# A four-layer graph network on one core: layer 3's edge numbers in fp32r, layer 0's split by a rounding copy, layer 1's norm on GpSimd

## The chip, the core and the metric

The kernel runs on one core of a Trainium2 chip. A core has five engines that each work through an instruction queue of their own, in order: PE (TensorE, matrix products into the accumulators, PSUM), DVE (VectorE, elementwise work and reductions), ACT (ScalarE, activations and copies), POOL (GpSimd, elementwise work in the on-chip memory SBUF) and SP (which starts transfers). They wait for each other by semaphores. The metric is the device time of one execution in microseconds; lower is better.

## The reference, cut to what matters

The input x is 32 graphs of 512 nodes with 128 features, and adj is one 512 x 512 matrix of zeros and ones. Each of four layers computes `x = x + layer(relu(layernorm(x)), adj)`, and layer 3 gives the result without the sum:

```python
# layer 3: every edge takes its weight from a list by its running number
m = adj > 0
idx = jnp.cumsum(m.reshape(-1).astype(jnp.int32)) - 1
vals = e[0][idx].reshape(adj.shape)          # e has 256 entries
A = jnp.where(m, vals, NEG)
A = jax.nn.softmax(A, axis=1)
out = (A * I) @ h0 + (A * (1 - I)) @ h1 + bias   # h0, h1: two projections
```

An edge number past the end of the list takes the last entry, so only the first 256 edges, counted row by row over the whole matrix, have an entry of their own. All of this depends on adj and e alone, so it is done once for all 32 graphs.

Layer 0 is an attention whose scores are built from pairs of nodes; for the nodes of the second half, its sum runs over a mask of zeros and ones. Layer 1 is an attention followed by a two-layer perceptron with norms. Layer 2 is a plain masked attention with an elu.

## The kernel before, in words

**Tiling.** A graph is four blocks of 128 nodes. Most tiles are 128 partitions by 4 x 128 values. A product of 128 x 128 by 128 x n in fp32 appears in the profile as two PE instructions. A product whose two operands are typed fp32r appears as one[...].

**The plan.** The function `tile_gnn_stack_kernel` does not emit instructions in the order of its text. It hands operations to `Plan.op`, each with an engine, an assumed length, the values it reads and writes, and, by the argument `port`, a note that DVE and POOL should not run marked instructions at the same time. `Plan.run` then chooses, step by step, the operation that can begin first by the assumed lengths, and fixes that order on every engine. A changed length, a changed number of buffers or a dropped operation can so move instructions anywhere. Buffers come from rooms (`by_pool`, `by_act`, `by_dve`, `scored`, `scores`, `turned`, `spare`, and the eight PSUM banks). The assumed lengths set the order only; on the chip, an engine runs its queue as its semaphores allow.

**The order of the work.** Per graph there is one chain of operations for each of the layers 0 to 3, with lags of 0, 4, 9 and 12 graphs, so that in the middle of the kernel four graphs are in work, one in each layer. Two more chains stand beside them: `prepare` (weights and masks) and `prepare_last` (layer 3's attention matrix), which fill gaps in the first rounds.

**The norm.** `preln(b, engine)` takes means and variances on DVE (L494, L496), the inverse deviation on POOL (`ve` L506, the power L508), and the normalised tile either on ACT (L528, with a shift made on DVE, L524) or on POOL (L543, with a shift made on ACT, L539). Then PE transposes it and ACT makes `hT`. Layers 0, 2 and 3 use POOL, layer 1 uses ACT.

**Layer 0's mask terms.** The values `hs2` have to be multiplied with the mask in fp32r, so they are split into a high and a low part, side by side in one tile `hl`. DVE cuts the last bits away (`cut`, L792), ACT copies the cut values to the high half (L805), POOL subtracts them from `hs2` for the low half (L806), and PE multiplies both halves at once (L828).

**Layer 3's preparation, `prepare_last`.**
- `up` is a triangle of ones; PE multiplies it with the transposed mask (L1106, bf16, 512 columns each), which counts the edges of a row up to each column. DVE copies the counts to `num` (L398) and a row's total to `row_n` (L1114).
- PE adds the totals of the rows before (L1121); DVE takes `row_lo` and `row_hi`, the first and last number of each row, and adds `row_lo` to `num` (L1134). From here `num` is the running number over the whole matrix.
- `in_row` says for each of the 256 list entries in which row it falls (L1159, L1160). PE gathers the numbers of these rows (`pg`, L1172). DVE compares (`ge`, L1176), takes the difference of neighbouring columns (L1181, L1182) and multiplies it with e (L1183). That is `e_at`, which holds each entry at its column.
- PE transposes `in_row` and spreads `e_at` to the rows (`pd`, L1194).
- DVE writes the last entry where the number is past the list (L1200), adds `pd` (L1204) and the mask (L1208) and takes the maximum (L1211). ACT takes the exponential (L1215), DVE divides (L1222) and takes the diagonal out (L1228 to L1230). PE transposes the result into `offT`, and the diagonal is spread into `adiag_rep`. Layer 3 uses both for every graph (L955, L970).

`e_at` and the transposed `in_row` have their place in `offT` until that is filled.

Of the kernel before, what the change touches and what calls it, by code (L numbers as in the profile page):

```python
# [37 lines left out]
P = 128  # L38
# [210 lines left out]
def kernel(  # L249
# [64 lines left out]
    scored = room("scored", 5, (P, C, P2))  # L314
    scores = room("scores", 8, (P, C, P))
    turned = room("turned", 4, (P, C, P))
    spare = room("spare", 9, (P, C, P))
# [195 lines left out]
    def preln(b, engine):  # L513
# [6 lines left out]
        if engine is ACT:  # L520
# [13 lines left out]
            op(ACT, 1.16, norm, [shift, rstd, v_x[b]], [xn])  # L534
# [135 lines left out]
    def layer0(b):  # L670
# [109 lines left out]
        def emit_rs2():  # L780
# [10 lines left out]
        cut = value(by_dve, "cut")  # L791
        op(DVE, 0.35, lambda: nc.vector.tensor_scalar(  # L792
            cut.t.bitcast(I32), hs2.t.bitcast(I32), -4096, None, ALU.bitwise_and), [hs2], [cut], port=1)
# [9 lines left out]
        for hf in range(H):  # L803
            own = slice(hf * H, hf * H + H)
            op(ACT, 0.31, lambda hf=hf, own=own: nc.scalar.copy(hl(hf)[:, :, 0, :], cut.t[:, own, :]), [cut], [hi[hf]])  # L805
            op(POOL, 0.7, lambda hf=hf, own=own: nc.gpsimd.tensor_sub(  # L806
                hl(hf)[:, :, 1, :], hs2.t[:, own, :], cut.t[:, own, :]), [hs2, cut], [lo[hf]], port=1)
# [39 lines left out]
    def layer1(b):  # L847
        hT, _ = preln(b, ACT)
        h = project_scored(hT, w1_ext, [v_w1])
        src, v_h = Value(), Value()  # L850
# [206 lines left out]
    def prepare_last():  # L1057
# [30 lines left out]

# [4 lines left out]
        for kb in range(C):  # L1093
            dve(0.31, lambda kb=kb: nc.vector.tensor_scalar(
                maskT_t(kb), adjT[:, kb, :], 0.0, None, ALU.is_gt), v_adjT, [maskT[kb]])
        num = [value(spare, "num") for _ in range(C)]
        row_n, row_lo, row_hi, nmax3, sum3, rsum3 = (
            const(n, (P, C)) for n in ("row_n", "row_lo", "row_hi", "nmax3", "sum3", "rsum3")
        )
        v_n, v_lo = Value(), Value()  # L1100
        for ib in range(C):
            pn = value(banks, "pn")

            def emit_pn(ib=ib, pn=pn):
                for kb in range(C):
                    nc.tensor.matmul(  # L1106
                        wide(pn.t), lhsT=maskT_t(kb)[:, blk(ib)],
                        rhs=up_t()[:, N - P - kb * P : 2 * N - P - kb * P],
# [3 lines left out]
            op(PE, 0.9, emit_pn, [*maskT, up], [pn])  # L1112
            copy_op(DVE, 0.6, lambda ib=ib: wide(num[ib].t), lambda pn=pn: wide(pn.t), [pn], [num[ib]])
            dve(0.1, lambda ib=ib: nc.vector.tensor_copy(row_n[:, ib : ib + 1], wide(num[ib].t)[:, N - 1 : N]),  # L1114
                [num[ib]], [v_n])
# [10 lines left out]
        op(PE, 1.5, emit_pb, [bf, v_n], [pb])  # L1126

        def emit_lo():
            nc.vector.tensor_copy(row_lo, pb.t[:, 0, 0:C])
            nc.vector.tensor_add(row_hi, row_lo, row_n)  # L1130

        dve(0.2, emit_lo, [pb, v_n], [v_lo])
        for ib in range(C):
            dve(0.31, lambda ib=ib: nc.vector.tensor_scalar(  # L1134
                wide(num[ib].t), wide(num[ib].t), row_lo[:, ib : ib + 1], None, ALU.add), [v_lo], [num[ib]])
# [18 lines left out]
        for ib in range(C):  # L1154
            ge_lo = value(spare, "ge_lo")

            def emit_in(ib=ib, ge_lo=ge_lo):
# [3 lines left out]
                    in_row_t(ib), rank, row_hi[:, ib : ib + 1], ge, ALU.is_lt, ALU.mult  # L1161
# [4 lines left out]
        e_at = offT[:, 0:KE, :]  # L1166
        in_rowT = offT[:, KE : 2 * KE, :]
        v_e_at, v_in_rowT = [Value() for _ in range(KE)], [Value() for _ in range(KE)]
        for kb in range(KE):
            pg = value(banks, "pg")  # L1170
            for ib in range(C):
                op(PE, 0.86, lambda kb=kb, ib=ib, pg=pg: nc.tensor.matmul(  # L1172
                    wide(pg.t), lhsT=in_row_t(ib)[:, blk(kb)], rhs=wide(num[ib].t),
                    start=(ib == 0), stop=(ib == C - 1)), [in_row[ib], num[ib]], [pg])
            ge = value(spare, "ge")
            dve(0.6, lambda kb=kb, pg=pg, ge=ge: nc.vector.tensor_scalar(  # L1176
                wide(ge.t), wide(pg.t), next_k[:, kb : kb + 1], None, ALU.is_ge), [pg, v_next], [ge])

            def emit_e(kb=kb, ge=ge):
                g = wide(ge.t)  # L1180
# [114 lines left out]
```

## Time and profile before

Three runs took 1076.15, 1074.54 and 1074.25 us; the median is 1074.54.

| | us |
|---|---|
| median of the runs | 1074.54 |
| profiled execution | 1074.58 |
| its span, first to last instruction | 1072.5 |
| PE busy | 1042.8 |
| DVE busy | 891.1 |
| ACT busy | 800.1 |
| POOL busy | 740.1 |

How to read the lines. A group line names the source line, the engine, the operation, the tile it writes and the tiles it reads, the shapes and the count; then the busy time in us and the mean of one in ns; then the idle time of the engine just before these instructions, and what ended it. A chain line has a start in us, a length in us, an engine, a tile and a line: the chain follows the work that ended last back from the end, at each step to what released it. PE products are pipelined and their ends are modelled, so a PE that is busy all the time is not of necessity at its peak, and the distance between starts says more than the length of one.

### The profile page before, as it was taken

The page shows a single profiled execution, that of the slowest core. Times are in us where ns is not written, and L with a number is a line of the kernel's source. Part 1 is how long each engine was busy: PE and PEld are TensorE (multiplying, and loading weights), DVE is VectorE, ACT ScalarE, POOL GpSimd, SP SyncE. Part 2 cuts the span into 40 slices and gives each one's busy share as a digit, 9 for nine tenths or more (in the row PEclk, how much of TensorE's full clock was granted, in tenths as well). Part 3 has the DMA queues.
Part 4 walks back from the last instruction along what each step waited for, and adds up shares of the span by engine and source line. Part 5 has one row for each costly group of instructions (what it writes and reads, how often), then busy time and mean ns, then how long its engine had stood idle before and what let it go on. Part 6 is the DMA issues. An engine that isn't in the chain of part 4 may idle for free.

```text
span 1072.5 us, 24953 instructions
## 1 busy us (share of the span) xinstructions
PE 1042.8 (97%) x8333; PEld 953.6 (89%) x8333; DVE 891.1 (83%) x3772; ACT 800.1 (75%) x2068; POOL 740.1 (69%) x1040
## 2 busy tenths in 40 slices
PE   6899999999999999999999999999999999999996
PEld 5786888889899999999999999999998999999995
DVE  7999999999988888888888889888887877876562
ACT  3577779887877777887777788877777878777571
POOL 7467546778677778877777787777767766657544
PEclk8899999999999999999999999999999999999998
DMA  7300000000000000000000000000000000000000
GB/s 183 82 1 2 1 2 11 12 11 21 2 21 21 21 21 21 21 1 21 21 21 11 12 11 2 12 11 11 11 11 11 12 9 13 11 11 16 16 25 25
DMA packets 56910, 20.47 MB, mean 19 GB/s; under 512 B 21584, under 2 KB 56272, under 8 KB 56784
## 3 DMA queue, kind: packets, MB, share of 16 engines
q1 hardware_dynamic: 56784, 18.90, 7.4%
q8 instruction: 66, 1.08, 0.4%
q14 instruction: 60, 0.49, 0.2%
HBM read 10.43 MB, written 8.39 MB: 18 GB/s over the span
## 4 chain that ended last, share of the span: by engine, by line
PE 77%; DVE 14%; ACT 3%; SPq 2%; POOL 2%; DMA 2%; issue 1%; DVEq 0%; ACTq 0%; POOLq 0%
PE po L658 18%; PE pt L405 14%; PE po L970 11%; PE pg L897 8%; PE proj L578 6%; PE po L823 4%; PE prow L405 3%; PE p L564 3%; PE po L966 3%; PE px L564 3%; DVE y L605 2%; PE pz L564 2%; DVE st L494 2%; PE po L828 2%; DVE pT L647 2%; SPq L389 1%
## 5 line engine op out<-in xcount | busy, mean ns | idle before, releaser
L658 PE MATMUL po<-h,pT 128*128 128x128 f32 x2048 | 240.8, 275 | 0.3
L658 PEld LDWEIGHTS po<-h,pT 128*128 128x128 f32 x2048 | 234.4, 192 | 1.5 <-ACT pT L396 0.5
L543 POOL TENSOR_SCALAR xn<-xs,shift,rstd 128x128 f32<-128x128 f32 x384 | 179.2, 480 | 11.4 <-ACT shift L539 9.6
L638 ACT ACTIVATE y<-y,nmax 128x512 f32<-128x512 f32 x256 | 181.6, 713 | 2.6 <-DVE nmax L620 2.2
L508 POOL TENSOR_TENSOR rstd<-ve,mhalf 128x4 f32<-128x4 f32 x160 | 166.0, 1038 | 13.3
L605 DVE CUSTOM_DVE_ANT_0 y<-prow,bias 128x512 f32<-128x512 f32 x256 | 163.1, 683 | 2.2 <-PE prow L405 2.2
L970 PE MATMUL po<-h,offT 128*128 128x128 f32 x1024 | 136.0, 276 | 0.7 <-ACT h L396 0.7
L897 PE MATMUL pg<-adjTe,hg 128*128 128x512 f32 x256 | 131.2, 594 | 0.4 <-DVE ge L1176 0.4
L405 PE MATMUL pt<-ident,y 128*128 128x128 f32 x1024 | 129.2, 273 | 1.9 <-ACT y L638 1.6
L405 PEld LDWEIGHTS pt<-ident,y 128*128 128x128 f32 x1024 | 115.2, 141 | 17.7 <-ACT y L638 9.8
L970 PEld LDWEIGHTS po<-h,offT 128*128 128x128 f32 x1024 | 125.1, 193 | 1.2 <-ACT h L396 1.2
L494 DVE BATCH_NORM_STATS2 st<-xs 128x6 f32<-128x128 f32 x512 | 110.2, 276 | 5.6 <-POOL xs L948 2.8
L578 PE MATMUL proj<-w_ext,hT 128*128 128x130 f32 x768 | 103.8, 278 | 1.4 <-ACT hT L553 1.4
L578 PEld LDWEIGHTS proj<-w_ext,hT 128*128 128x128 f32 x768 | 95.5, 192 | 9.5 <-issue 4.8
L630 ACT ACTIVATE y<-y,src 128x512 f32<-128x512 f32 x128 | 85.3, 717 | 22.4 <-DVE rmax L605 18.3
L843 POOL TENSOR_TENSOR xs<-xs,rest 128x256 f32<-128x256 f32 x32 | 23.5, 736 | 113.3 <-DVE top L616 82.3
L553 ACT ACTIVATE hT<-pt 128x512 f32<-128x512 f32 x128 | 75.0, 590 | 33.3 <-PE pt L405 18.4
L396 ACT COPY h<-proj 128x260 f32<-128x260 f32 x192 | 66.1, 372 | 32.1 <-PE proj L578 30.2
L630 ACT ACTIVATE y<-y,h 128x512 f32<-128x512 f32 x128 | 82.6, 713 | 7.4 <-DVE rmax L605 7.3
L405 PE MATMUL pt<-ident,xn 128*128 128x128 f32 x512 | 79.4, 275 | 6.8 <-POOL xn L543 6.3
L647 DVE TENSOR_TENSOR pT<-pt,adjT 128x512 f32<-128x512 f32 x128 | 83.4, 677 | 1.5 <-PE pt L405 1.5
L405 PEld LDWEIGHTS pt<-ident,xn 128*128 128x128 f32 x512 | 61.5, 141 | 25.7 <-POOL xn L543 10.1
(189 smaller groups left out, 2331.5 us busy)
## 6 DMA issues: line engine op xcount, KB each, us to landing
xs<-in_x_dram SPq DMA_DIRECT2D x32, 256.0 KB, 3.9
out_dram<-yo SPq DMA_DIRECT2D x32, 256.0 KB, 2.3
u<-h SPq DMA_DIRECT2D x128, 0.5 KB, 1.8
bias<-in_adj_dram SPq DMA_DIRECT2D x4, 256.0 KB, 4.0
wts<-in_L_gnn_W_dram SPq DMA_DIRECT2D x3, 64.0 KB, 3.8
rows<-in_L_gnn_bias_dram SPq DMA_DIRECT2D x2, 64.0 KB, 3.7
wt_o<-L_gnn_others_weight_dram SPq DMA_DIRECT2D x1, 64.0 KB, 2.6
wts<-n_L_gnn_self_weight_dram SPq DMA_DIRECT2D x1, 64.0 KB, 4.1
```

Of the source, the lines that this page charges most:

```text
L405: nc.tensor.transpose(dst(k), src(k), ident)
L494: nc.vector.bn_stats(st[:, c, :], src(c))
L508: nc.gpsimd.tensor_tensor(rstd.own, ve, mhalf, ALU.pow)
L543: nc.gpsimd.tensor_scalar(xn.t[:, c, :], src[:, c, :], shift.own[:, c : c + 1], rstd.own[:, c : c + 1], ALU.add, ALU.mult,)
L578: nc.tensor.matmul(p[:, c, :], lhsT=column(hT, 2 * k + c), rhs=w_ext, start=True, stop=True)
L605: nc.vector.tensor_tensor_reduce(wide(y[ib].t), wide(prow.t), bias[:, ib, :], 1.0, LOWEST, ALU.add, ALU.max, rmax.own[:, ib : ib + 1],)
L630: nc.scalar.activation(yw, yw, AF.Prelu, alpha=0.2, bias=src()[:, ib : ib + 1])
L638: nc.scalar.activation(yw, yw, AF.Exp, bias=nmax.own[:, ib : ib + 1], accum_out=ssum[0].own[:, ib : ib + 1])
L647: op(DVE, 0.6, lambda ib=ib, pt=pt, pT=pT: nc.vector.tensor_mul(pT.t, pt.t, weights[:, :, blk(ib)]), [pt, *v_weights], [pT])
L658: nc.tensor.matmul(po[ib].t[:, ib, :], lhsT=pT.t[:, jb, :], rhs=h[0].t[:, jb, 0:P], start=(jb == 0), stop=(jb == C - 1),)
L897: nc.tensor.matmul(wide(pg.t), lhsT=hg.t[:, nb, :], rhs=adjTe[:, nb, :], start=(nb == 0), stop=(nb == C - 1))
L970: nc.tensor.matmul(po[ib].t[:, ib, :], lhsT=offT[:, jb, blk(ib)], rhs=h1.t[:, jb, :], start=False, stop=(jb == C - 1),)
```

## The change

- **Layer 3's numbers stay within their row.** `num` is no longer made a running number over the whole matrix. `row_lo` goes into the thresholds instead: a new small product `pk` brings each entry's `row_lo` to `first_k`, against which the gathered counts are compared, and `last_lo` is the row's own threshold for the last entry. Counts within a row are at most 512.
- **Single fp32r passes.** `num`, `in_row`, `e_at` and the transposed `in_row` are written as fp32r, and the gathering and spreading products run in it. So that e keeps its precision it is split in two terms, `e_hi` and `e_lo`, and the spreading product runs over both. The counting product streams only the columns that the triangle doesn't leave at zero.
- **Other engines.** ACT copies `num` out of PSUM. POOL takes the difference of neighbouring columns (into `adiag_rep`, which is free until the end) and adds the mask. Adding `pd` and taking the maximum are one DVE instruction. The softmax is built in `offT`, not in `num`, and `e_at` and the transposed `in_row` have tiles of their own in `spare`.
- **Layer 0.** The cut on DVE goes. ACT's copy to fp32r reads `hs2` itself and rounds, and POOL subtracts the rounded values.
- **Layer 1.** `preln` is called with POOL. The value `v_h` holds its tile's buffer.
- **Rooms.** `scored` has 6 buffers instead of 5, `spare` 8 instead of 9. Some assumed lengths differ.

```diff
-    scored = room("scored", 5, (P, C, P2))
+    scored = room("scored", 6, (P, C, P2))
...
-    spare = room("spare", 9, (P, C, P))
+    spare = room("spare", 8, (P, C, P))
...
-            op(ACT, 1.16, norm, [shift, rstd, v_x[b]], [xn])
+            op(ACT, 1.54, norm, [shift, rstd, v_x[b]], [xn])
...
-        cut = value(by_dve, "cut")
-        op(DVE, 0.35, lambda: nc.vector.tensor_scalar(
-            cut.t.bitcast(I32), hs2.t.bitcast(I32), -4096, None, ALU.bitwise_and), [hs2], [cut], port=1)
...
-            op(ACT, 0.31, lambda hf=hf, own=own: nc.scalar.copy(hl(hf)[:, :, 0, :], cut.t[:, own, :]), [cut], [hi[hf]])
+            op(ACT, 0.31, lambda hf=hf, own=own: nc.scalar.copy(hl(hf)[:, :, 0, :], hs2.t[:, own, :]), [hs2], [hi[hf]])
             op(POOL, 0.7, lambda hf=hf, own=own: nc.gpsimd.tensor_sub(
-                hl(hf)[:, :, 1, :], hs2.t[:, own, :], cut.t[:, own, :]), [hs2, cut], [lo[hf]], port=1)
+                hl(hf)[:, :, 1, :], hs2.t[:, own, :], hl(hf)[:, :, 0, :].bitcast(F32)), [hs2, hi[hf]], [lo[hf]], port=1)
...
     def layer1(b):
-        hT, _ = preln(b, ACT)
+        hT, _ = preln(b, POOL)
         h = project_scored(hT, w1_ext, [v_w1])
-        src, v_h = Value(), Value()
+        src, v_h = Value(), Value(h[0].slot)
...
                     nc.tensor.matmul(
-                        wide(pn.t), lhsT=maskT_t(kb)[:, blk(ib)],
-                        rhs=up_t()[:, N - P - kb * P : 2 * N - P - kb * P],
+                        wide(pn.t)[:, kb * P :], lhsT=maskT_t(kb)[:, blk(ib)],
+                        rhs=up_t()[:, N - P : 2 * N - P - kb * P],
...
-            copy_op(DVE, 0.6, lambda ib=ib: wide(num[ib].t), lambda pn=pn: wide(pn.t), [pn], [num[ib]])
+            copy_op(ACT, 0.59, lambda ib=ib: num_t(ib), lambda pn=pn: wide(pn.t), [pn], [num[ib]])
...
-        for ib in range(C):
-            dve(0.31, lambda ib=ib: nc.vector.tensor_scalar(
-                wide(num[ib].t), wide(num[ib].t), row_lo[:, ib : ib + 1], None, ALU.add), [v_lo], [num[ib]])
+            nc.vector.tensor_scalar(last_lo, row_lo, -1.0, NE + 1.0, ALU.mult, ALU.add)
...
+        def emit_terms():
+            nc.vector.tensor_copy(e_hi, e_col)
+            nc.vector.tensor_sub(e_lo, e_col, e_hi.bitcast(F32))
...
+        def emit_pk():
+            for kb in range(KE):
+                for ib in range(C):
+                    nc.tensor.matmul(
+                        pk.t[:, 0, kb : kb + 1], lhsT=in_row_t(ib)[:, blk(kb)], rhs=row_lo[:, ib : ib + 1],
+                        start=(ib == 0), stop=(ib == C - 1),
+                    )
...
+                    nc.tensor.matmul(
+                        wide(pg.t), lhsT=in_row_t(ib)[:, blk(kb)].bitcast(F32R), rhs=num_t(ib),
+                        start=(ib == 0), stop=(ib == C - 1),
+                    )
...
-                wide(ge.t), wide(pg.t), next_k[:, kb : kb + 1], None, ALU.is_ge), [pg, v_next], [ge])
-
-            def emit_e(kb=kb, ge=ge):
-                g = wide(ge.t)
-                nc.vector.tensor_copy(e_at[:, kb, 0:1], g[:, 0:1])
-                nc.vector.tensor_sub(e_at[:, kb, 1:], g[:, 1:], g[:, 0 : N - 1])
-                nc.vector.tensor_scalar(e_at[:, kb, :], e_at[:, kb, :], e_col[:, kb : kb + 1], None, ALU.mult)
+                wide(ge.t), wide(pg.t), first_k[:, kb : kb + 1], None, ALU.is_ge), [pg, v_first], [ge])
+
+            def emit_at(ge=ge):
+                nc.gpsimd.tensor_copy(adiag_rep[:, 0:1], wide(ge.t)[:, 0:1])
+                nc.gpsimd.tensor_sub(adiag_rep[:, 1:], wide(ge.t)[:, 1:], wide(ge.t)[:, 0 : N - 1])
+
+            def emit_e(kb=kb):
+                for t, e in enumerate((e_hi.bitcast(F32), e_lo)):
+                    nc.vector.tensor_scalar(e_at_t(t, kb), adiag_rep, e[:, kb : kb + 1], None, ALU.mult)
...
+                for t in range(2):
+                    for kb in range(KE):
+                        nc.tensor.matmul(
+                            wide(pd.t), lhsT=wide(in_rowT[kb].t).bitcast(F32R)[:, blk(ib)], rhs=e_at_t(t, kb),
+                            start=(t == kb == 0), stop=(t == 1 and kb == KE - 1),
+                        )
...
+            def emit_mask(ib=ib):
+                a = offT[:, ib, :]
+                nc.gpsimd.tensor_add(a, a, bias[:, ib, :])
...
+                nc.vector.tensor_tensor_reduce(a, wide(pd.t), a, 1.0, LOWEST, ALU.add, ALU.max, top)
+                nc.vector.tensor_scalar(nmax3[:, ib : ib + 1], top, -1.0, None, ALU.mult)
```

## The prediction

> **What bounds the kernel now.** I read the page first (engine totals), then the table of busy time by stretch, then the chain of work that ended last, then the groups of instructions inside the stretch that the chain points to.
>
> ```profile
> PE 1042.8 (97%) x8333; PEld 953.6 (89%) x8333; DVE 891.1 (83%) x3772; ACT 800.1 (75%) x2068; POOL 740.1 (69%) x1040
> ```
>
> PE at 97% suggests that only PE work counts. The stretches (columns: length, then busy time and instruction count of PE, PEld, DVE, ACT, POOL, the granted clock, DMA) say when that is so:
>
> ```profile
> 40.00:160.00 120.00, 115.32 (x794) 95.36 (x794) 117.49 (x505) 86.85 (x247) 68.01 (x95) 0.97 0.04 6
> 160.00:300.00 140.00, 138.47 (x1100) 125.30 (x1100) 130.62 (x579) 118.64 (x318) 103.78 (x146) 1.00 0.06 15
> 300.00:800.00 500.00, 500.00 (x4123) 466.47 (x4123) 421.18 (x1824) 397.09 (x1031) 374.15 (x514) 1.00 0.06 14
> 1000.00:1072.50 72.50, 61.97 (x512) 58.92 (x510) 33.83 (x109) 30.29 (x69) 36.24 (x54) 0.94 0.08 23
> ```
>
> From 300 to 800 us PE never pauses; 4123 instructions in 500 us are 8.25 per us. From 40 to 160 us it runs 6.6 per us, and DVE is the fuller engine: 117.5 of 120 us. That is the stretch in which layer 3's preparation runs between the first batches. The chain there, a few of its pieces in order of time:
>
> ```profile
> 126.03 0.60 DVE num L1204
> ...
> 128.51 0.60 DVE num L1208
> ...
> 133.97 0.60 DVE nmax L1211
> ...
> 138.87 0.33 DVE cut L792
> ```
>
> Adding the chain's pieces by engine in the six stretches of 20 us from 40 to 160 gives DVE 15.5, 18.3, 18.1, 13.8, 20.2 and 14.0: 99.9 of 120 us. Preparation and cuts stand in it. So the kernel has a start whose last wait is DVE's, a long middle that is PE's alone, and a tail of 72.5 us with PE 85% busy. Before 40 us the chain is DMA and SP's queue.
>
> **Part 1: layer 3's edge numbers, PE.** Rates come from the chain at 300 us:
>
> ```profile
> 300.20 0.86 PE pg L897 x2
> 301.06 0.44 PE prow L405 x4
> 301.50 0.48 PE po L828 x4
> ```
>
> A 512-column fp32 product is two instructions, 0.86 us. Four 256-column fp32r products take 0.48, so 0.12 each, 0.47 ns per column; 512 columns then cost 0.24 (estimate from that row). The gathering product (L1172): 8 x 0.86 = 6.9 becomes 8 x 0.24 = 1.9, so -5.0. The spreading product (L1194): 6.9 becomes 16 x 0.24 = 3.8, because e is split in two terms, so -3.0. The counting product (L1106) streams 1280 columns per row block in place of 2048: 16 x 192 x 0.47 ns = -1.4, at 20 to 28 us, under the DMA chain. Added: 8 one-column fp32 products (pk), 16 instructions; nearest row the one-column products at L1121, 20 in 2.3 us, so +1.8. Sum -7.6, of which -6.2 in the stretch from 40 to 160.
>
> **Part 2: the same, DVE, ACT, POOL.** The rows, taken from 20 to 160 us:
>
> ```profile
> L792 DVE TENSOR_SCALAR cut<-hs 128x512 int32<-128x512 int32 x9 | 3.7, 416 | 0.0
> L1208 DVE TENSOR_TENSOR num<-num,bias 128x512 f32<-128x512 f32 x4 | 2.7, 680 | 0.0
> L1211 DVE TENSOR_REDUCE nmax<-num 128x1 f32<-128x512 f32 x4 | 2.7, 678 | 0.0
> L1134 DVE TENSOR_SCALAR num<-num,row_lo 128x512 f32<-128x512 f32 x4 | 2.4, 613 | 0.0
> L1182 DVE TENSOR_TENSOR offT<-ge 128x511 f32<-128x511 f32 x2 | 2.4, 1182 | 0.0
> ```
>
> Off DVE go L1134 (2.4), L1182 with its first-column copy L1181 (2.4 + 0.3), L1208 (2.7) and L1211 (2.7): 10.5. On come two more products with e (0.486 each by L1183: 1.0), the add that becomes add-with-maximum (L605: 0.683 + 0.082 for its read-out, against 0.670: +0.4 over four), four negations of one column (0.154 by L1018: 0.6), and four small ones (last_lo, first_k, the two terms, about 0.16 each: 0.6): 2.6. The copies out of PSUM (L398, 4 x 0.678 = 2.7) move to ACT at 4 x 0.59, but at 30 to 35 us, where ACT was 45% busy and the chain is DMA's; I count nothing for them, and up to 2.7 if DVE's queue carries its lead past 40 us.
>
> POOL gets four mask adds (1.28 each, as L958) and two differences with their first column (1.28 + 0.3): 8.3 us. They lie on the way from ge to e_at and from num to the softmax; POOL was 57% busy there. Should that cover go, layer 3 starts late, but it is first needed at 245.7 us, by layer 3's own-term product on DVE (L955), some 80 us behind.
>
> **Part 3: the cut in layer 0.** Eight cuts lie in 40 to 160: 8 x 0.416 = -3.3 on DVE. ACT's rounding copy takes the place (0.402, as before, now from hs2), and POOL's subtraction now waits for ACT instead of DVE. Behind that POOL instruction stand, by the order, a batch's four norm pieces and hn's add; PE's mask products wait for it. Between nothing and one ACT activation (0.72) per batch; I take 0, since the copy can start 0.4 earlier than before.
>
> **Part 4: layer 1's norm.** ACT loses 4 x 0.485 per batch and gains a shift of 0.20; DVE loses its shift (6 x 0.163 = 1.0 in the stretch); POOL gains 4 x 0.48 = 1.92.
>
> ```profile
> L543 POOL TENSOR_SCALAR xn<-xs,shift,rstd 128x128 f32<-128x128 f32 x384 | 179.2, 480 | 11.4 <-ACT shift L539 9.6 <-DVE res L923 1.2
> L528 ACT ACTIVATE xn<-xs,shift,rstd 128x128 f32<-128x128 f32 x128 | 52.5, 485 | 1.4 <-PE px L564 0.8 <-DVE shift L524 0.6
> ```
>
> In the middle a round of the four layers takes 31.03 us (in the chain, a group of layer 1's third products begins at 338.95 and the next one at 369.98 us). POOL: 374.15/500 x 31.03 = 23.2, plus 1.92, is 25.1; DVE 26.1 falls to 25.6; ACT 24.6 to 22.9. Nobody reaches 31.03, so nothing is charged there. Cover gone, 1 us of late norm per round would be 1 us of PE.
>
> [...] By the rows: DVE's two-SBUF-input update L924 takes 0.695 on average, its PSUM-fed product L647 0.677; 0.02 apart, with POOL 57 to 75% busy, and the plan keeps marked instructions of the two apart. I charge 1 us of the 10.7, and keep it for the range.
>
> The room changes (scored 6, spare 8) cost nothing by themselves; the instructions of the start come in another order, and PE's last 136 products stand in the same order as before, so I let the tail keep its length.
>
> **The sum.** DVE in the stretch: -10.5 + 2.6 - 3.3 - 1.0 = -12.2, so 117.5 becomes 105.3. PE: 115.3 - 6.2 = 109.1 by busy time[...]. Two engines this full do not interleave perfectly; the stretch now lasts 2.5 over its fuller engine. DVE 105.3 + 2.5 + 1 (port) = 109; PE's own bound is about the same. 120 - 109 = 11; I take off 1 for the reordered start. The profiled execution was 1074.58 (span 1072.5 and 2.08 around it), 0.04 over the median, which changes nothing: 1074.5 - 10 = 1064.5.
>
> **Rivals.** *Both shares count in part* (15%): PE's saving alone converts, or half of DVE's, because latencies fill the holes: 3 to 6 us, about 1070. For: PE stands at 115 of 120 too. Against: the chain there is 83% DVE.
> *More* (8%): the 3.1 us taken from DVE at 20 to 40 us move the start as well, and the stretch from 160 to 300, DVE at 93%, shortens: 1058.
> *No change* (8%): [...]12.2 - 10.7 = 1.5 us left: 1073.
> *Slower* (8%): layer 1's norm becomes late in the middle. It stands in POOL's in-order queue with two other batches' norms and behind their power instructions (1.04 each); where it ends after PE reaches its transposes, PE stops in every round. 0.7 us in each of 32 rounds is 22, less the 10: 1087. It decides from 0.3 us per round. Against: from 300 to 800 PE waited for no POOL norm, though three layers take theirs from it, and POOL idles 5 us per round for layer 0's rest.
>
> **How the numbers follow.** My own case (the stretch gives 6 to 14 us: 1060.5 to 1068.5) has 61%. Faster: 61 + 15 + 8 = 84%. A measurement of this kernel tells 0.2% (2.1 us) from no change; within that 8%, slower 8%. The range runs from 1058.5, half of *more*, to 1072.5, all of *in part*, and leaves out *slower*, most of *no change* and the far end of *more*: 20%.
>
> **What would show it.** After: gathering and spreading products in single instructions of 0.24 spacing; DVE without L1134, L1208, L1211 and cuts; the stretch between the first layer-0 products and PE's saturation shorter by about 10; the same 31.03 us round in the middle, without PE waits on xn; POOL near 81% there. Wrong if PE shows idle time before layer 1's transposes, if two-input DVE rows grow beyond 0.7, or if the start is as long as now with DVE below 95%.

## The result and the profile after

The changed kernel takes 1075.51 us (median of 12 runs, 1071.82 to 1077.78); the kernel before takes 1074.29 (12 runs, 1073.12 to 1076.15). The ratio is 1.0005 with a 95% interval of 0.9992 to 1.0019: no difference that can be measured. The prediction was 1064.5, with a range of 1058.5 to 1072.5. It was wrong: the gain of 10 us didn't come. The changed kernel also spreads more than the one before: its single runs differ by 6 us.

The profiled execution of the changed kernel took 1077.78 us, with a span of 1076.0, and is the slowest of its twelve. Three lines of its page: the engine totals, the granted clock of TensorE in 40 slices, and the chain by engine.

```profile
PE 1045.5 (97%) x8341; PEld 965.0 (90%) x8341; DVE 871.7 (81%) x3702; ACT 763.4 (71%) x1976; POOL 796.4 (74%) x1176
...
PEclk8698999999999999999999999999999999999998
...
PE 85%; POOL 5%; DVE 5%; issue 2%; ACT 1%; DMA 1%; SPq 0%; POOLq 0%; DVEq 0%; ACTq 0%
```

The clock and the chain of the kernel before:

```profile
PEclk8899999999999999999999999999999999999998
...
PE 77%; DVE 14%; ACT 3%; SPq 2%; POOL 2%; DMA 2%; issue 1%; DVEq 0%; ACTq 0%; POOLq 0%
```

DVE has 19 us less to do (891.1 before) and POOL 56 us more (740.1 before). In the chain, DVE's share falls from 14% to 5%, and PE and POOL have taken its place. The second digit of the clock is new. It was 8 before and is 6 now: between 27 and 54 us the trace has TensorE at half of its clock for 20.5 us (27.0 to 40.6 and 47.5 to 54.3).

The table of busy time by stretch, as it was shown of before (length, busy time and count of PE, PEld, DVE, ACT, POOL, granted clock, DMA share, GB/s):

```profile
40.00:160.00 120.00, 111.29 (x794) 98.11 (x794) 111.15 (x505) 79.71 (x234) 88.72 (x126) 0.94 0.03 4
160.00:300.00 140.00, 139.87 (x1119) 127.33 (x1118) 129.12 (x556) 114.03 (x301) 110.61 (x160) 1.00 0.06 14
300.00:800.00 500.00, 499.98 (x4113) 466.25 (x4112) 413.28 (x1787) 375.01 (x978) 387.77 (x577) 1.00 0.06 14
1000.00:1076.00 76.00, 64.91 (x529) 61.31 (x527) 36.38 (x115) 33.23 (x75) 37.41 (x54) 0.95 0.07 22
```

From 40 to 160 us no engine is full any more: PE is at 111.3 (115.3 before) and DVE at 111.2 (117.5 before). Yet just as many PE instructions pass as before, 794. A part of what was taken off the two engines has become idle time on both. In the middle, PE is as full as before, with 4113 instructions per 500 us (4123 before).

The tail is longer. The last 502 PE instructions, in the kernel before and then in the changed one:

```profile
1001.70:1072.50 70.80, 60.27 (x502) 57.70 (x500) 33.14 (x108) 28.59 (x65) 35.52 (x54) 0.94 0.08 23
```

```profile
1003.60:1076.00 72.40, 61.31 (x502) 58.19 (x501) 34.30 (x108) 29.63 (x67) 36.68 (x54) 0.95 0.08 23
```

Both do the same products, and the changed kernel takes 1.6 us more for them.

The prices of the single instructions were right. Of the changed kernel, the groups from 20 to 160 us, and one piece of its chain:

```profile
L1249 POOL TENSOR_TENSOR offT<-offT,bias 128x512 f32<-128x512 f32 x4 | 5.1, 1271 | 0.4 <-DVE offT L1243 0.4
...
L1254 DVE CUSTOM_DVE_ANT_0 offT<-pd,offT 128x512 f32<-128x512 f32 x4 | 2.7, 684 | 0.0
...
L1212 POOL TENSOR_TENSOR adiag_rep<-ge 128x511 f32<-128x511 f32 x2 | 2.1, 1035 | 0.0
```

```profile
97.88 0.94 PE pd L1235 x4
```

Four spreading products take 0.94, so 0.235 each (0.24 foretold); POOL's mask add takes 1.271 (1.28), its difference 1.035 (1.28), and the add with maximum 0.684 (0.683).

What PE waits for in the changed kernel from 40 to 160 us, from the view of waits (line, what it waited for, us in all, times, the longest):

```profile
PE po L825 <- POOL hl L803: 1.9, 3, 1.5
PE prow L405 <- DVE ltn L737: 1.6, 1, 1.6
PE prow L405 <- DVE ls L695: 1.4, 1, 1.4
PE pt L405 <- POOL xn L543: 1.2, 3, 0.7
```

And a part of its chain, where POOL carries it:

```profile
67.41 1.40 POOL hl L803 x2
68.80 1.74 POOL xn L543 x4
70.54 1.24 POOL offT L1249
71.78 1.96 POOL xn L543 x4
73.74 0.70 POOL xs L840
...
81.22 0.70 POOL hl L803
...
81.96 1.48 PE po L825 x4
```

POOL, to which the prediction gave its new work for nothing, is busy 19.50 of the 20 us from 60 to 80. Its queue holds the norms, the new mask adds and layer 0's low halves one behind the other, and at 80.45 us PE stands still for 1.5 us until the last of these is there. That made three suspects: POOL's queue; the order, which the plan chose anew; and the clock, which the trace records as granted at half for 34.1 us before 100 us (13.7 us in the kernel before). Half clock for 20.5 us more is 10.2 us of TensorE's full speed, about the size of the gain that is missing. But this profile is of the slowest run, and its mean clock, 0.980, is the lowest of the twelve. Their average is 0.986, that of the kernel before 0.991 in its runs beside the experiments: on the average run, 0.005 of 1075 us, some 5 us of full speed.

### The profile page after: what moved, and what is told of

Its sections match the earlier page's. It is cut to its first block, busy times and chain, and to the rows that moved or that the text cites. A ratio compares the mean times of both kernels' runs of the same rounds, so it can differ in the third digit from the quotient of the medians.

```text
span 1076.0 us, 24957 instructions
## 1 busy us (share of the span) xinstructions
PE 1045.5 (97%) x8341; PEld 965.0 (90%) x8341; DVE 871.7 (81%) x3702; ACT 763.4 (71%) x1976; POOL 796.4 (74%) x1176
## 4 chain that ended last, share of the span: by engine, by line
PE 85%; POOL 5%; DVE 5%; issue 2%; ACT 1%; DMA 1%; SPq 0%; POOLq 0%; DVEq 0%; ACTq 0%
PE po L658 20%; PE pt L405 16%; PE po L967 10%; PE pg L894 9%; PE proj L578 7%; PE po L820 5%; PE prow L405 3%; PE p L564 3%; PE po L825 2%; PE px L564 2%; PE pz L564 2%; PE po L963 2%; POOL xn L543 2%; PE po L817 1%; PE po L830 1%
## 5 line engine op out<-in xcount | busy, mean ns | idle before, releaser
L543 POOL TENSOR_SCALAR xn<-xs,shift,rstd 128x128 f32<-128x128 f32 x512 | 230.9, 466 | 2.8 <-PE pt L405 1.2
L508 POOL TENSOR_TENSOR rstd<-ve,mhalf 128x4 f32<-128x4 f32 x160 | 169.7, 1061 | 13.3
L405 PE MATMUL pt<-ident,y 128*128 128x128 f32 x1024 | 133.8, 275 | 0.5 <-DVE pT L647 0.2
L578 PEld LDWEIGHTS proj<-w_ext,hT 128*128 128x128 f32 x768 | 99.4, 197 | 17.7 <-issue 9.0
L578 PE MATMUL proj<-w_ext,hT 128*128 128x130 f32 x768 | 106.1, 282 | 1.9 <-ACT hT L553 1.7
L939 POOL TENSOR_TENSOR v<-v,rows 128x512 f32<-128x512 f32 x32 | 40.8, 1274 | 71.4 <-DVE v L938 71.4
L945 POOL TENSOR_TENSOR xs<-xs,em 128x512 f32<-128x512 f32 x32 | 41.9, 1309 | 69.4 <-DVE em L944 63.3
L405 PE MATMUL pt<-ident,xn 128*128 128x128 f32 x512 | 82.2, 279 | 7.2 <-POOL xn L543 6.2
L396 ACT COPY h<-proj 128x260 f32<-128x260 f32 x192 | 65.0, 371 | 20.5 <-PE proj L578 18.1
```

The source lines that it names most:

```text
L405: nc.tensor.transpose(dst(k), src(k), ident)
L508: nc.gpsimd.tensor_tensor(rstd.own, ve, mhalf, ALU.pow)
L543: nc.gpsimd.tensor_scalar(xn.t[:, c, :], src[:, c, :], shift.own[:, c : c + 1], rstd.own[:, c : c + 1], ALU.add, ALU.mult,)
L578: nc.tensor.matmul(p[:, c, :], lhsT=column(hT, 2 * k + c), rhs=w_ext, start=True, stop=True)
```

## The experiments

Times are medians. Ratios are to the kernel before, run beside each on the same chip (1074.08 to 1074.33 us).

### Parts taken back, or made alone

Each of the first two runs is the changed kernel with one part taken back; the third takes back both, which leaves layer 3's part and the rooms; the fourth is the kernel before with the norm and the rooms only.

```diff
 # e1: layer 1's norm back on ACT
-        hT, _ = preln(b, POOL)
+        hT, _ = preln(b, ACT)
 # e2: layer 0's cut back on DVE (cut, L792; ACT and POOL take cut again)
+        op(DVE, 0.35, lambda: nc.vector.tensor_scalar(
+            cut.t.bitcast(I32), hs2.t.bitcast(I32), -4096, None, ALU.bitwise_and), [hs2], [cut], port=1)
...
 # e3: both of these edits to the changed kernel
 # e4: the kernel before, with
+    scored = room("scored", 6, (P, C, P2))
+    spare = room("spare", 8, (P, C, P))
...
+        hT, _ = preln(b, POOL)
...
+        src, v_h = Value(), Value(h[0].slot)
```

> The changed kernel with one word put back: layer 1's norm on ACT (as before), layer 3's and layer 0's parts as changed. Theory POOL: between 40 and 110 us the changed kernel's POOL is the fullest engine (19.5 of 20 us at 60 to 80), and the norm's pieces are 14 of its 30 there; without them POOL has room, the start no longer runs late, and the time falls to 1066 +- 2. Theory clock: what cost the gain is TensorE at half clock for 34 us of the first 100 us (14 us before), made by gaps that any reordered start has; then the half-clock time stays near 30 us and the time near 1074.[...]

> The changed kernel with layer 0's cut on DVE put back, the norm on POOL and layer 3's part as changed. Theory POOL: the norm stays, so no gain: 1075 to 1078 (DVE has its 0.42 per graph again, hidden). A theory that the rounding copy, and POOL's wait for ACT behind it, ate the gain: 1066.

> Layer 3's part and the rooms alone: norm on ACT and cut on DVE as before. Theory POOL: 8.3 us of new POOL work in the start (mask adds, differences) against 10.7 us of norm that are gone; DVE loses 7.9 us and PE 7.6: 1068 +- 2. Theory clock or reordering: 1072 to 1076, with over 25 us at half clock in the first 100.

> The kernel before with layer 1's norm on POOL (its tile held, scored 6 and spare 8 as in the change), nothing else changed. Theory POOL: the norm alone makes the start longer and nothing else shorter: 1077 to 1081, POOL over 85% busy at 60 to 100 us. Theory clock: 1074 unless the half-clock time in the first 100 us grows over 14 us. If moving the norm is harmless: 1074.

| | us | ratio, interval |
|---|---|---|
| norm back on ACT | 1093.76 | 1.0193 [1.0168, 1.0218] |
| cut back on DVE | 1094.14 | 1.0184 [1.0171, 1.0197] |
| layer 3's part alone | 1092.02 | 1.0164 [1.0151, 1.0177] |
| norm alone | 1078.29 | 1.0041 [1.0028, 1.0055] |

All four are slower than both kernels. The profiled execution of the last run took 3799 us, far from its other five, so only its times are read. No expectation named a number near 1092. The fourth's 1077 to 1081 came true, but by luck: the rooms alone, without the norm, take 1079.99 (below).

No part has a price of its own here: all three together cost nothing, any two or one of them up to 20 us. Putting the cut back, 0.416 us of DVE's work for each graph and 3.3 in the start, can't cost 18.6 us by the work in it; from 300 to 800 us PE waits for nothing in that run. Each version gets a new order from the plan, and the orders differ by more than the work does. Where the norm is back on ACT, a part of the loss lies in the middle: from 300 to 800 us PE is busy 497.8 and 496.5 us. With the cut back, one wait in the first 160 us is longer than the whole edit there. The view of waits of that run:

```profile
PE pk L1189 <- DVE in_row L1163: 4.8, 1, 4.8
```

The plan has put the new small product `pk` (L1186 in the changed kernel) so early on PE's queue that everything behind it stands for 4.8 us.

### The order alone

The kernel before with nothing but the new rooms: every instruction is the same, only their order differs.

```diff
-    scored = room("scored", 5, (P, C, P2))
+    scored = room("scored", 6, (P, C, P2))
...
-    spare = room("spare", 9, (P, C, P))
+    spare = room("spare", 8, (P, C, P))
...
-        src, v_h = Value(), Value()
+        src, v_h = Value(), Value(h[0].slot)
```

> The kernel before with only the buffer counts of the change (scored 6, spare 8, layer 1's tile held by the added value): no instruction added or removed, only the plan's order differs. Theory order (the plan's order alone moves the time by more than the work that the change takes away): more than 4 us off 1074. If order is harmless: 1074 +- 1.

It took 1079.99 us, ratio 1.0049 [1.0036, 1.0061]: 5.7 us for the order alone. Its stretch from 40 to 160 us, and its largest wait there:

```profile
40.00:160.00 120.00, 109.42 (x753) 89.50 (x752) 117.12 (x495) 81.92 (x236) 70.24 (x95) 0.99 0.03 4
```

```profile
PE po L823 <- DVE hs L788: 5.6, 3, 3.0
```

DVE is as full as in the kernel before (117.1 against 117.5), but 753 PE instructions pass in place of 794. The same view of the kernel before has this wait at 2.2 us:

```profile
PE po L823 <- DVE hs L788: 2.2, 2, 1.3
```

DVE's busy time is the same in both; what differs is the order of its queue, and with it how long PE waits for `hs`. The clock isn't the cause: before 100 us this run has 10.2 us at half clock, the kernel before 13.7. So a full DVE doesn't say how long the stretch is.

### The work alone

The other way round: the order of the kernel before, kept on every engine, with the work left out that the change removes. DVE's adds of `row_lo` and of the mask, the maximum (one column each in their place), the differences and layer 0's cuts are gone, and three of four gathering and one of two spreading products. The output is then not the reference's.

```diff
-                wide(num[ib].t), wide(num[ib].t), row_lo[:, ib : ib + 1], None, ALU.add), [v_lo], [num[ib]])
+                wide(num[ib].t)[:, 0:1], wide(num[ib].t)[:, 0:1], row_lo[:, ib : ib + 1], None, ALU.add), [v_lo], [num[ib]])
...
-                op(PE, 0.86, lambda kb=kb, ib=ib, pg=pg: nc.tensor.matmul(
+                op(PE, 0.86, lambda kb=kb, ib=ib, pg=pg: ib == 0 and nc.tensor.matmul(
...
```

> The order of the kernel before, instruction for instruction on every engine, with the work that my sum takes away left out. On DVE the running-number add, the mask add and the maximum run over one column, the column difference and layer 0's cut are left out: about 12 us less in 40 to 160 us. On PE 10 of the 16 gathering and spreading products are left out, 8.6 us. The output is not the reference's. Theory sum (the accounting is right and the new order is what failed): 1064 +- 3. Theory that the start is bound by latencies and not by DVE's and PE's amounts of work: above 1070.

It took 1070.85, ratio 0.9966 [0.9954, 0.9979]. By the prediction's own sum this kernel should have won 10 to 12 us; it won 3.5. Its stretch from 40 to 160 us:

```profile
40.00:160.00 120.00, 110.15 (x785) 94.26 (x784) 111.70 (x508) 88.86 (x251) 67.10 (x98) 0.96 0.04 6
```

The clock there is nearly that of the kernel before (0.97), and neither engine is full. Nothing was added to POOL or ACT here and nothing was moved, so most of the missing gain isn't the price of what the change adds.

### The clock

The changed kernel, its order kept, with filler products (128 x 128, values never read) ahead of its three pauses of 1.4 to 1.5 us: before `pc_w` at 25.3, before graph 4's `prow` at 47.3, and before graph 4's mask products at 80.5 us. The first of them, from the view of waits of the changed kernel (the other two are shown above):

```profile
PE pc_w L416 <- issue: 1.5, 1, 1.5
```

```diff
+    def fill(own, n=5):
+        for _ in range(n):
+            nc.tensor.matmul(own, lhsT=ident, rhs=ident, start=True, stop=True)
...
+            if b == 4:
+                fill(prow.t[:, 0, :])
```

> The changed kernel in its own order, with five filler products (0.22 us each) put on PE ahead of each of three waits in the start: before the score-weight product at 25 us, before layer 0's row transposes of graph 4 at 47 us and before its mask products at 80 us; their results are overwritten. Theory clock (pauses of 1.4 us at these places drop TensorE to half clock for 6.8 us each): half-clock time in the first 100 us falls from 34 to below 20 us and the time by 4 to 8, to 1068 to 1071. Theory POOL: 3.3 us more PE work or nothing, 1075 to 1078.

It took 1070.40 (1070.01 to 1071.12), ratio 0.9960 [0.9948, 0.9973]: 5.1 us less than the changed kernel, though PE does 3.3 us more. It is the fastest version here that leaves no work out, ahead of both kernels. The half clock before 100 us is 6.8 us in its profile, 34.1 in that of the changed kernel. The stretches of the changed kernel, and then of this one:

```profile
20.00:40.00 20.00, 18.20 (x102) 17.13 (x101) 15.80 (x90) 9.19 (x27) 15.24 (x30) 0.67 0.62 150
40.00:60.00 20.00, 17.46 (x120) 16.24 (x119) 17.17 (x89) 11.04 (x41) 10.69 (x17) 0.81 0.05 2
60.00:80.00 20.00, 18.79 (x147) 16.97 (x146) 20.00 (x99) 12.39 (x38) 19.50 (x29) 1.00 0.08 15
80.00:100.00 20.00, 17.93 (x114) 15.84 (x114) 16.74 (x72) 12.77 (x37) 17.78 (x28) 0.83 0.01 1
```

```profile
20.00:40.00 20.00, 19.23 (x150) 17.91 (x147) 18.24 (x108) 11.07 (x34) 18.39 (x34) 0.91 0.69 151
40.00:60.00 20.00, 17.33 (x133) 15.29 (x133) 19.69 (x104) 12.96 (x50) 14.51 (x22) 1.00 0.05 2
...
80.00:100.00 20.00, 18.67 (x124) 15.23 (x125) 19.84 (x89) 12.82 (x34) 19.33 (x31) 1.00 0.02 2
```

PE looks busy in both, 18.2 and 19.2 of 20 us from 20 to 40; but at a clock of 0.67 the first gets through 102 instructions and the second through 150, ten of them the five fills. Busy time at half clock is little more than half work: the 16 products `proj` from 28.74 us take 3.67 us in the changed kernel, at half clock, and 2.03 from 29.38 us in the kernel before, at full clock.

How much of the 5.1 us is the clock's can be read from the runs as well. Within the twelve runs of the changed kernel the time falls by 5.35 us for each 0.01 of mean clock (1077.78 at 0.980, 1071.82 at 0.990; correlation -0.73). Their mean is 0.986, that of the five runs with fills 0.9934, so 0.0074 more, which by this slope is 4.0 us. That is a correlation and an estimate, but it needs no other version.

The control is the kernel before with 18 fillers at three of its own pauses:

```diff
+                if ib == 0 and b in (1, 3,):
+                    fill(own)
...
+            if first_fill:
+                fill(pt.t[:, 0, :], 8)
```

> The kernel before, with every engine's order kept, and 18 filler products of 128 x 128 (about 4 us of PE, values never read) ahead of three of its pauses: the first transposes of layer 0 (2.54 us at 12.0) and the second and fourth graph's products with hs (1.29 us at 44.2, 0.91 at 62.1). Theory 'the half clock that the changed kernel's early pauses draw is what the change lost': the kernel before has 13.7 us at half clock in its start, of which the fills can take at most 6.8 us of capacity; I expect 1071 to 1073, and never as much as the 5.1 us that the fills brought in the changed kernel. Rival 'fills make any order of this kernel about 4 us faster': 1070, the same as the changed kernel with its fills, and then the change itself is worth nothing even at a full clock.

1073.89 (13 runs), ratio 0.9996 [0.9987, 1.0004]: nothing that can be measured. Neither number that the expectation gave was right. So fills don't make any order 4 or 5 us faster. But the control moves the clock only a little. The mean clock of its runs is 0.9926, that of the kernel before beside them 0.9904: 0.0022 more, where the fills of the changed kernel brought 0.0074. Its profiled execution, with 3.4 us at half clock in the start in place of 13.7, is one of its fast ones: 1072.47, 2.1 us less than the profiled one of the kernel before. So it isn't shown that the clock is worth nothing in the kernel before; that kernel has less of it to win back.

### POOL

The changed kernel in its order, with POOL relieved of some 15 us in the start: the first six norms of layer 1 computed by ACT at the same place of the plan, and the mask adds on one column. The values are then not the reference's.

```diff
-        hT, _ = preln(b, POOL)
+        hT, _ = preln(b, POOL, b < 6)
...
-                nc.gpsimd.tensor_add(a, a, bias[:, ib, :])
+                nc.gpsimd.tensor_add(a[:, N - 1 :], a[:, N - 1 :], bias[:, ib, N - 1 :])
```

> The changed kernel in its own order, with POOL's new work in the start taken off its queue: the norm pieces of layer 1's first six graphs are issued to ACT at the same place (with a shift that is not scaled, so their values are not the reference's), and the mask adds run over one column. POOL loses 15 us in the first 200. Theory POOL (POOL at 19.5 of 20 us holds the start): 1066 to 1070. Theory clock: what the pauses do, so near 1075 if the pauses at 25, 47 and 80 us stay.

1074.65 (13 runs), ratio 1.0000 [0.9991, 1.0009]. POOL falls from 19.50 to 12.69 of 20 us between 60 and 80, and the time stays. POOL carried the chain there, but it isn't what the gain was lost to: the half clock from 27 to 41 us, which comes before it, stands in this run as in the changed kernel (a mean clock of 0.67 from 20 to 40 us in both). The one from 81.6 us is gone (1.00 from 80 to 100 us, against 0.83). What POOL's work would cost at a full clock was not run.

### Which engine's saving counts

The order of the kernel before, 31 filler products at five pauses, and the work left out on both engines, on DVE alone, and on PE alone (the outputs are then not the reference's, as in the run with the work left out).

```diff
+                if ib == 0 and b in (1, 3, 5,):
+                    fill(own)
...
+                if b == 0 and nb == 0:
+                    fill(pg.t[:, 0, :], 8)
...
```

> The kernel before in its own order with the work of the change left out (as in the run of that name: about 12 us of DVE's work and 8.6 us of PE's; the output is then not the reference's), and 31 filler products (about 7 us of PE) ahead of its pauses at 12.2, 42.8, 59.4, 83.7 and 100.5 us. It took 1070.85 without the fills. Theory 'the work taken out turned into waits between engines, and those waits have no clock to win back': 1069 to 1071. Rival 'the sum was right and the half clock ate it': 17 us at half clock are 8.5 us of capacity, so 1063 to 1066.

> The kernel before in its own order, with the 31 filler products at five pauses and only DVE's work left out (about 12 us, layer 3's adds, differences and maximum and layer 0's cuts; the output is then not the reference's). With DVE's and PE's work out and the same fills it took 1068.75, 5.3 below the kernel before. The prediction's rule (the stretch lasts 2.5 us over its fuller engine, and DVE is the fuller one): with PE's products back PE's busy time is the bound, and about 4 us are won, 1070. 'DVE's saving alone carries it': 1069, the same as with both. 'PE's saving alone carries it': 1073 to 1074, the same as the fills alone.

> The same order and fills, with only PE's products left out (three of four gathering and one of two spreading products, 10 of 512 columns, about 8.6 us of PE; the output is then not the reference's), and all of DVE's work in place. The prediction's rule (DVE was the fuller engine) gives nothing over the fills alone: 1073.9. 'PE's saving carries it': 1069. If each of the two alone brings 2 to 3 us, the stretch is bound by chains in which both engines take turns, and neither engine's total tells its length.

| left out, with fills | us | ratio, interval | less than the fills alone |
|---|---|---|---|
| nothing (the 18 fills of the control) | 1073.89 | 0.9996 [0.9987, 1.0004] | |
| 8.6 us of PE | 1072.81 | 0.9989 [0.9981, 0.9997] | 1.1 |
| 12 us of DVE | 1070.85 | 0.9965 [0.9953, 0.9977] | 3.0 |
| both | 1068.75 | 0.9950 [0.9936, 0.9964] | 5.1 |

The stretch from 40 to 160 us of the run with DVE's work out, then of the one with both out:

```profile
40.00:160.00 120.00, 119.12 (x861) 101.34 (x860) 112.61 (x515) 89.46 (x253) 68.73 (x101) 0.99 0.04 6
```

```profile
40.00:160.00 120.00, 114.88 (x852) 99.17 (x851) 114.50 (x516) 91.83 (x259) 69.83 (x103) 0.99 0.04 6
```

The first row has 18 fills and the others 31, since the control was not run with 31. Neither saving counts in full. DVE's alone gives 3.0 us, a quarter. PE's alone, 1.1, isn't clear of the noise, as its interval overlaps that of the fills alone; with DVE's work already out, PE's products bring another 2.1 (1070.85 to 1068.75). With DVE's work alone out PE is busy 119.1 of 120 us, some 5 us of it with fills, so the fills may hide a part of what DVE's saving is worth. The two single runs lie near what the expectations worked out from the prediction's rule (1070 and 1073.9) and don't refute it; the run with both out and no fills does. With both out and fills, 1068.75 is just below the 1069 to 1071 of the first theory and far from its rival's 1063 to 1066.

With both out and fills, the clock is at 0.99 and both engines stand at 114 to 115 of 120 us, so neither is full. What is left are short waits in many places. The largest of PE and of DVE there:

```profile
PE prow L405 <- ACT h L396: 1.2, 2, 0.7
```

```profile
DVE hn L897 <- POOL rstd L890: 1.9, 3, 1.2
```

### What holds the clock down

In the kernel before, TensorE's clock falls to half at 43.26 us and is back at 50.09. PE had not paused since 38.26 us. Its instructions ahead of the fall, from the view of them in order of time:

```profile
38.75 0.60 PE L405 MATMUL prow<-ident,ls 128*128 128x128 f32 x4
39.19 2.29 PE L1121 MATMUL pb<-row_n,bf 128*128 128x1 f32 x20
41.34 1.14 PE L578 MATMUL proj<-w_ext,hT 128*128 128x130 f32 x8
42.31 1.47 PE L405 MATMUL pt<-ident,xn 128*128 128x128 f32 x4
```

The 20 products `pb` (L1121 before, L1123 after) are one column wide. In the changed kernel they lie at 32.2 to 36.5 us, within the 13.7 us at half clock. That they bring the clock down like a pause was a guess. Two more runs of the changed kernel in its order test it: with eight fills between these products only, and with the fills at the three pauses as well.

```diff
             for ib in range(C):
+                fill(pb.t[:, 1, :], 2)
                 for kb in range(ib + 1):
```

> The changed kernel, every engine's order kept, with 8 filler products of 128 x 128 (about 1.8 us of PE at full clock, values never read) between the 20 one-column products pb at 32 to 36 us, and none at the pauses. Theory 'one-column products count as idle for the clock': the half clock that the pause at 25.3 us starts at 27.0 ends at 33.8 in place of 40.6 (6.8 us in place of 13.7), and the time falls by 0 to 2 us below the changed kernel's, to 1073.5 to 1075.5. Rival 'only the pauses count': the 13.7 us stay, and the time rises by up to 1.8 us.

> The changed kernel with fills at its three pauses, as in the earlier run (1070.40), and between the 20 one-column products as well. Theory 'one-column products count as idle for the clock': the 3.4 us at half clock that followed those products at 33.2 us in the earlier run are gone, only the first one near 16 us stays; the time is 1069 to 1071, since the fills cost 1.8 us of PE and give back 1.7. Rival 'only the pauses count': the half clock at 33 us stays, as nothing paused before it, and the time is 1071 to 1072.

With fills in `pb` alone, half clock takes 3.4 us of the stretch from 27 to 41 us in place of 13.6 (clock 0.76 and 1.00 of 7 us each, against 0.50 and 0.53). The table of busy time of the changed kernel, then of that run:

```profile
27.00:34.00 7.00, 7.00 (x35) 7.00 (x35) 5.82 (x32) 4.33 (x11) 4.01 (x7) 0.50 0.73 189
34.00:41.00 7.00, 7.00 (x35) 7.00 (x36) 3.29 (x14) 0.20 (x1) 5.57 (x11) 0.53 0.43 94
```

```profile
27.00:34.00 7.00, 6.78 (x47) 6.81 (x47) 5.94 (x37) 4.80 (x14) 5.59 (x11) 0.76 0.76 179
34.00:41.00 7.00, 6.94 (x61) 6.75 (x61) 5.00 (x21) 1.18 (x3) 5.51 (x10) 1.00 0.41 90
```

The expectation was 6.8 us, so a part of the fall is more than its theory gives; these are single profiles. The runs agree: the mean clock of the 14 with fills in `pb` is 0.9908, that of the changed kernel's 0.986. With the fills at the pauses alone, the clock is 0.94 from 27 to 34 us and 0.81 from 34 to 41; with all fills it is 1.00 in both, but 0.94 from 40 to 60 and 0.97 from 60 to 80 us, where it was 1.00. So fills between these products took half clock away there in both runs. Why they do was not shown.

For the time it is worth little. With fills in `pb` alone it is 1074.03, ratio 0.9998 [0.9988, 1.0008], not to be told from the changed kernel: the eight fills are about 1.8 us of PE, and take up most of what the clock gives back. With all fills it is 1071.64, ratio 0.9980 [0.9971, 0.9989], 1.2 us more than with the fills at the pauses alone. Its mean clock, 0.9928, is no higher than the 0.9934 there, so these fills cost their time and give nothing back.

## Why the prediction was wrong, point by point

- **The prices of the instructions: right.** Single passes at 0.235, the rows gone from DVE, POOL's new pieces at or below their price.
- **"The stretch now lasts 2.5 over its fuller engine": this step failed.** It took a nearly full DVE for a bound that moves as DVE's work shrinks. In the old order, at nearly the old clock, 12 us of DVE and 8.6 us of PE gave 3.5 us, not 11; with the fills in both, 5.1. The chain, 83% DVE, named the engine that is late most often, but a queue in a fixed order is late by where an instruction stands in it. Where DVE got shorter, the next wait was another engine's: with both out, PE's largest is on ACT's `h`, DVE's on POOL's `rstd`. This is the mechanism of the rival *in part*, which had 15%; its 3 to 6 us hold the measured 3.5 and 5.1. The result itself has the number of the rival *no change*, but 10.7 us of DVE held off by POOL, its cause, is not what the runs show.
- **"The room changes cost nothing by themselves": failed.** The rooms alone cost 5.7 us. The "1 for the reordered start" can't be checked by itself within the whole change, since every version has an order of its own. At a good clock, the changed kernel (1070.40) stands 1.7 us behind the bare removal of the work in the old order (1068.75); that holds the order, POOL's new work and the norm.
- **"I let the tail keep its length": failed, by 1.6 us.** The same 502 PE instructions take 72.4 us at the end of the changed kernel, 70.8 before. With fills at the pauses they take 72.6, with the work out and fills 70.6: this alone is the size of the 1.7 us above, so the start leaves next to nothing for the new order and POOL's work. The last 136 products do stand in the same order as before and take 29.4 us in both; the loss comes ahead of them. The two versions with the norm back on ACT take 72.5, so it isn't the norm's move; what it is stays open.
- **The clock: not in the sum at all.** Against the changed kernel with fills it took 5.1 us, by the slope of the runs 4.0. The kernel before doesn't have that clock either: against its 0.991, the changed kernel's 0.986 is some 2.7 us by the same slope (an estimate). The page before showed the clock below 1 in the first slices and the tail, and I read past it. I took PE's products at the price that they have at full clock, and no step asked what new pauses of PE would do to the clock.
- **POOL counted at nothing in the start: right in time.** POOL did get on the chain, but taking 15 us off it changed nothing.
- **1 us charged for POOL holding DVE off: right in size.** The 10.7 of which it was taken were my estimate of the worst case, 24 new POOL pieces of 0.447 us each at full length; no run shows such a price. From 20 to 160 us the wide products with two SBUF inputs, `hs`, went from 680 and 682 ns to 686 and 698, 18 of them in all. Two small ones grew more: `rs` from 166 to 276 ns, nine times, and `nmax` of L620 from 136 to 252, five times. That is 1.8 us in all at most. POOL as the cause isn't shown: with POOL relieved, the two small rows stand at 277 and 339, and one of the wide ones at 734.
- **Layer 1's norm free in the middle: right.** No wait of PE from 300 to 800 us. From the 7000th to the 500th PE instruction before the end the changed kernel takes 794.6 us, the kernel before 795.1, for the same products. The rival *slower* didn't come.

In one line: 1064.5 foretold; 4.3 for work that turns into waits (1068.75); 1.7 for the rest of the change, nearly all of it in the tail (1070.40); 5.1 for what the fills at the pauses win back, most of it clock (1075.51). These are differences of medians from several chips, each uncertain by more than 1 us. The 4.3 is low if anything, as 1064.5 held 2 us for POOL beside DVE and for the reordering, which the run behind 1068.75 doesn't have.

## What to carry to other kernels

Where several engines are nearly full and hand work to each other in a fixed order, don't count a saving on the fullest one as time: leave the work out with the order kept, and see what it gives, before rewriting anything. Where a planner sets the order, compare versions with the order held fixed on every engine, as a change of buffers alone can cost more than the edit brings. Read TensorE's granted clock slice by slice beside its busy time: here two pauses of 1.5 us (at 25.3 and 80.5 us) came with 13.7 and 6.8 us at half clock, and a few products without use at the kernel's three pauses won 5.1 us. Read the mean clock of all runs as well, since one profile can be the slowest of them.

## What the runs showed of the hardware

- **Half clock is close to half speed.** At half clock (26.98 to 40.63 us of the changed kernel) 16 products `proj` took 3.67 us, and the 20 products `pb` 4.26; in the kernel before, at full clock, they took 2.03 and 2.29.
- **Pauses and the clock.** In the changed kernel PE paused from 25.28 to 26.75 us, and the clock was at half from 26.98 to 40.63; it paused from 80.45 to 81.96, and the clock was at half from 81.59 to 88.42. The half clock from 47.46 to 54.29 began 0.13 us into the pause of 1.37 us at 47.33. In the kernel before, a pause of 2.54 us up to 14.57 was followed by half clock from 15.96 to 22.78. With fills in the changed kernel's three pauses, 6.8 us at half clock were left before 100 us in place of 34.1.
- **Not every pause.** A pause of 1.61 us in the changed kernel (132.29 to 133.90) and one of 1.11 us in the kernel before (90.85 to 91.95) left the clock full.
- **A fall without a pause.** In the kernel before the clock fell at 43.26 us, 5.0 us after the end of PE's last pause, with the 20 one-column products at 39.19 to 41.48 us ahead of it. Fills between these products cut the half clock between 27 and 41 us of the changed kernel from 13.6 to 3.4 us.

What it is that brings the clock down, and how long a pause has to be, the runs don't show.
